# A four-layer graph network on one core: y's bank pair split by engine, layer 1's first maps placed behind the fourth chunk, and part of the fourth bank's sums put off

## The chip, the cores and the metric

The kernel runs on one core of one Trainium2 chip. The time is device microseconds for one execution. Three runs of the kernel before the change are known, and one more execution was taken by the hardware profiler. Engines are named as in the profile: PE is the matrix engine and PEld its weight loads, DVE the vector engine, ACT the scalar engine, POOL the general-purpose engine, and SP the engine that issues most transfers. All five have queues of their own[...].

## What is computed

The input x has 8 samples of 2048 nodes with 64 channels; adj is a 2048 x 2048 matrix. Four layers follow, each of the form "normalise, clamp at zero, run a graph layer, add to x":

```python
h = jnp.maximum(_layernorm(x, axis=-1), 0.0)
x = x + layer(h, adj)

# layer 0: three Chebyshev terms, weights of its own for every node
As = [I, A, 2 A @ A - I]
w = einsum('nd,dkio->nkio', embedding, weight)
out = einsum('bnki,nkio->bno', einsum('knm,bmc->bnkc', As, x), w) + embedding @ bias

# layer 1: three steps, node 0 of v replaced at the start
effects = einsum('nm,bmd->bnd', adj, v)
v = relu(concat([v, effects]) @ W1.T + b1) @ W2.T + b2

# layer 2: a weighted adj @ h, then a map.  layer 3: masked softmax attention over adj
```

Layer 0 is where y (its product with the node weights) is made, and layer 1's first step comes right behind it. These two places are what the change touches.

## The kernel before

**Data.** The main path (`uniform_path`) uses that every row of adj holds one value at its non-zero places: it keeps the signs as BT, 16 chunks of 128 nodes by 2048 columns, and multiplies the sums by a row of scales (`crow`). A float operand is split into a high part H (rounded) and a low part L (the rest), and a product with BT is two matmuls, one for each part, so 32 matmuls of 128x512 make one bank of 512 columns over all 16 chunks (`chunks`). There are four such banks (`NB`), and the 8 samples go in 4 pairs `p`. Layer 3's attention needs only sums in this path. A test of the matrix (`test`, `test_load`) runs beside layers 1: 64 pieces, each with a load `st`, a transposed load `mt` and one DVE operation `junk`, with three slots for the loads.

**The order of work.** Each engine's queue is fixed when the kernel is built. The kernel's `InOrder` wrapper ties the PE, and through layer 0's end and layer 1's first step all five engines, to the order in which the code issues; elsewhere a scheduler of the build places instructions by its own estimate of times. A tile of a pool comes free when the last reader of its former content is done.

**The y stage** (from line 1217, `apply_k`, `apply_w`, and the loop at line 1369) works through 16 groups `g` of 128 nodes. For each group the node weights are generated on the PE from the embedding E and the table wg (`make_w`, tiles `gen`, six steps of 16 matmuls, copied out by DVE and ACT in halves as `w<-gen`), and then applied to the three terms (`tt` holds the first two, `t2` or `t` the third) as matmuls of 32 columns into `yb`. In the loop step i of group g+1's `make_w` comes ahead of step i of group g's `apply_w`. Steps 0 to 2 of `apply_w` are the first half group (T = 0), steps 3 to 5 the second (T = 1). Step 0 or 3 applies the third term (`apply_k(.., 1)`), the two others the first two. A half group has two banks of sums, for the parities `par` of the output channels' halves. After step 2 or 5 they are copied to the tile `ys`; after step 5 four POOL transfers store `ys` to yD in memory. Beside it, in pieces, runs the normalisation for layer 1 of the first pair's first three blocks (`beside`).

The two banks of a half group are one tile `yb` of [128, 2, 512] with one buffer, and each of the two copies reads its half of the columns from both banks:

```python
for h in range(2):
    copy = (nc.scalar.copy, nc.vector.tensor_copy)[h]
    copy(to, yp[2].rearrange("p r (h x o) -> p h r x o", h=2, o=32)[:, h])
```

The last half group (g = 15, T = 1) takes two tiles of the pool `psg` instead, as `gen` tiles, and each engine then makes two copies of 256.

**Reload.** BT's room is used by the y stage, so 13 of its chunks (BT_A to BT_D) are loaded again at the stage's end as 16-bit values (`load_again`), and widened in place by ACT and DVE: `widen` copies the first half and the third quarter with the engine it is given, and the last quarter always with ACT. `by_act` names the chunks that ACT widens whole.

**Layer 1's first step** (`first_step`, line 1585) holds four banks of sums at once, in two tiles of two banks (`big`). In the first loop chunk m is added to all four banks, for m = 0 to 11, with H and L of the first three blocks (`H_u`, `L_u`). At m = 3 (`KEEP`) the last block (0,3) of the first pair gets its y added and is normalised (`x1_add`, `go_on`), with the widening of chunks 10 to 15 put between. At m = 8 `map_two(0)` is issued: eight matmuls `ph` from the tiles gT into two banks of the tag `tr`, whose four copies on ACT write gT back. After the loop the last block is transposed (`to_feat`: `pt_gT`, also of the tag `tr`), copied by ACT, mapped (`first_operand(3)`: `bn_u`) and split into H and L. Then each bank gets chunks 12 to 15 and is scaled by DVE (`scale`, result `g`), with `add` (a DVE add, a relu on ACT, two test pieces). In the third bank's turn come `map_two(2)` and `maps_two(0)` (`ph` and the 64 matmuls `bn`), the operand of the second step.

**Behind it**, in the second step, the blocks of the next pair are prepared through loads `acc`, `bn` (the bias), `yt` (the y of layer 0) on SP's queue, adds on DVE, a power (`rstd`) on POOL, stores `xs` and `hp` on POOL's queue. `acc` has two buffers; `sq` and `pl` share one.

Of the kernel before, what the change touches and what calls it, by code (L numbers as in the profile page):

```python
# [8 lines left out]
F32 = mybir.dt.float32  # L9
# [66 lines left out]
def uniform_path(  # L76
# [30 lines left out]
    nc = InOrder(tc)  # L107
    P = 128
    B, N, C = x.shape
    NP = B // 2  # L110
    NCH = N // P
    NB = N // 512
# [6 lines left out]
    psums = [pro.enter_context(tc.tile_pool(name="psump", bufs=1, space=bass.MemoryType.PSUM))]  # L119
# [11 lines left out]
    def bt(m):  # L131
        return BT[:, m] if m < KEEP else BTs[m - KEEP]
# [220 lines left out]
    def chunks(ps, hl, nb, ms, fill={}):  # L353
        for m in ms:
            for i in range(2):
                nc.tensor.matmul(
                    ps, hl[m // 4][i][:, m % 4, :], bt(m)[:, nb * 512:(nb + 1) * 512],
                    start=(m == 0 and i == 0), stop=(m == NCH - 1 and i == 1),
                )
            if m in fill:  # L360
                fill[m]()
# [271 lines left out]
    for m in range(NCH):  # L633
# [5 lines left out]
        if m % 2 and m < 12:  # L639
            k = m // 2 + 2  # L640
# [42 lines left out]
    for m in range(NCH):  # L683
# [14 lines left out]
        name="psumt", bufs=2, space=bass.MemoryType.PSUM, reuse_waits="tile"  # L698
# [127 lines left out]
    def first_operand(q):  # L826
        hl, gT = ops[0]
        hl.append(halves(back_whole(gT[q], w1e, f"u_{q}"), f"u_{q}"))
# [126 lines left out]
    def x1_load(p, nb):  # L955

        x1_rest(p, nb, *x1_first(p, nb))
# [19 lines left out]
    def x1_add(to=None):  # L977

        p, nb, acc, yt, bn = x1s.pop(0)
        nc.vector.tensor_tensor(  # L980
            nodes(acc), nodes(acc), bn[:, :, None, :].to_broadcast([P, 4, 2, C]), op=ALU.add
        )
        nc.vector.tensor_tensor(acc, acc, yt, op=ALU.add)
        keep(p, nb, acc, f"1_{p}_{nb}", b2r[:, None, None].to_broadcast([P, 4, 2, C]),
             lambda z, p, nb: to(z) if to else splits.append(lambda: store_planes(z, 1, p, nb)))
# [70 lines left out]
    for n, (kind, p) in enumerate(rounds):  # L1056
# [22 lines left out]
    hl = hl_of["b", 3]  # L1079
# [5 lines left out]
    psg = pgs.enter_context(tc.tile_pool(  # L1085
        name="psumg", bufs=4, space=bass.MemoryType.PSUM, reuse_waits="tile"
    ))
    psgs.append(psg)
    psl = pls.enter_context(tc.tile_pool(
        name="psuml", bufs=1, space=bass.MemoryType.PSUM, reuse_waits="tile"  # L1090
# [98 lines left out]
    for k in range(6):  # L1189
        make_w(0, k)  # L1190
        nb = 1 + k // 2
        for q in range(3 * (k % 2), 3 * (k % 2) + 3):
            m, i = order_l[NCH - KEEP + q // 2], q % 2
# [19 lines left out]
        name="psumy", bufs=1, space=bass.MemoryType.PSUM, reuse_waits="tile"  # L1213
# [3 lines left out]
    yps, yss = {}, {}  # L1217
# [29 lines left out]
    def apply_w(g, i):  # L1247

        T = i // 3
        if i in (0, 3):  # L1250
            if (g, T) == (NCH - 1, 1):
                yps[g, T] = [
                    psg.tile([P, 512], F32, tag="gen", name=f"yb_{g}_{T}_{par}") for par in range(2)
                ]
            else:
                yb = psums[-1].tile([P, 2, 512], F32, tag="yb", name=f"yb_{g}_{T}", bufs=1)
                yps[g, T] = [yb[:, 0], yb[:, 1], yb]
        u = 2 * T
        if i % 3 == 0:
            apply_k(g, u, 1)  # L1260
            apply_k(g, u + 1, 1)
        else:
            apply_k(g, u + i % 3 - 1, 0)
        if i in (2, 5):
            if T == 0:
                yss[g] = typ0.tile([P, 2, 4, 4 * C], F32, tag="ys", name=f"ys_{g}", bufs=2)
            ys, yp = yss[g], yps[g, T]
            for h in range(2):
                copy = (nc.scalar.copy, nc.vector.tensor_copy)[h]
                to = ys[:, h, 2 * T:2 * T + 2, :].rearrange("p s (j r o) -> p r (s j) o", j=4, r=2)  # L1270
                if len(yp) == 3:
                    copy(to, yp[2].rearrange("p r (h x o) -> p h r x o", h=2, o=32)[:, h])
                    continue
                for r in range(2):
                    copy(to[:, r], yp[r].rearrange("p (h x o) -> p h x o", h=2, o=32)[:, h])
            if T == 1:
                nb, t = divmod(g, 4)
                yr = ys.rearrange("(x j) h u f -> j x h u f", j=4)
                yd = yD[nb][:, :, :, t].rearrange("t b (j h u) c -> j (t b) h u c", h=2, j=4)
                for j in range(4):  # L1280
                    nc.gpsimd.dma_start(yd[j], yr[j][:, :, :, j * C:(j + 1) * C])
# [77 lines left out]

    shorts = {}  # L1360

    def widen(m, copy):

        to, src = shorts[m]
        for a, b in ((0, N // 2), (N // 2, 3 * N // 4)):
            copy(to[:, a:b], src[:, a:b])
        nc.scalar.copy(to[:, 3 * N // 4:], src[:, 3 * N // 4:])

    for g in range(NCH):
# [28 lines left out]
        name="psum", bufs=2, space=bass.MemoryType.PSUM, reuse_waits="tile"  # L1398
# [6 lines left out]
    for q in range(3):  # L1405
        first_operand(q)
    assert not splits
    by_act, by_dve = (3, 6, 9, 13), (4, 5, 7, 8, 10, 11, 12, 14, 15)
    for m in range(KEEP, 10):
        widen(m, nc.scalar.copy if m in by_act else nc.vector.tensor_copy)  # L1410

# [173 lines left out]
    def first_step(hl, gT, crow_of, g_new, hl_new, nm, map_two, maps_two, finish_two, scale, add):  # L1585

        two_ = [psums[-1].tile([P, 2, 512], F32, tag="big", name=f"bv2_{i}") for i in range(2)]
        sums = [two_[nb % 2][:, nb // 2] for nb in range(NB)]

        def crow(nb):  # L1590
            crow_of[nb] = load_crow(nb, f"{nm}_{nb}")

        crow(0)
        crow(1)
        for m in range(3 * NB):
            for nb in range(NB):
                chunks(sums[nb], hl, nb, (m,))
            if m == KEEP:
                x1_add(last_z.append)
                widen(10, nc.vector.tensor_copy)  # L1600
                go_on()
                widen(11, nc.vector.tensor_copy)
                go_on()
                for k in range(12, NCH):
                    widen(k, nc.scalar.copy if k in by_act else nc.vector.tensor_copy)
            if m == 2 * NB:
                map_two(0)
        ops[0][1].append(to_feat(last_z[0], feat(0, "gT_1_0_3"), "gT_1_0_3"))
        first_operand(3)
        x1_load(1, 0)  # L1610
        for _ in range(3):
            test_load()
        for nb in range(NB):
            chunks(sums[nb], hl, nb, range(3 * NB, NCH))
            scale(sums[nb], nb)
            if nb < 2:
                crow(nb + 2)
            if nb == 2:
                map_two(2)
                finish_two(0, maps_two(0))  # L1620
            add(nb)
            go_on()
        x1_load(1, 1)
        nc.on = ("gpsimd",)
        first_done.append(products[-1])
        later.extend((x1_behind, x1_behind))

        def put_off():
            ps = maps_two(2)
            return lambda: finish_two(2, ps)  # L1630

        carry.append(put_off)
        return hl_new, g_new
# [741 lines left out]
```

## Time and profile before

| | |
|---|---|
| time, median of three runs | 1145.01 us (1135.91, 1145.01, 1149.62) |
| the profiled execution | 1152.51 us, of which span 1150.4 us |
| mean granted PE clock | 0.972 |
| y stage, 291 to 505 us | PE busy 201.0 of 214.0 us, clock 0.97, DMA share 0.50 |
| 505 to 520 us | PE busy 11.0 of 15 us, clock 1.00, DMA share 0.75 |
| 530 to 545 us | PE busy 15.0 of 15 us, clock 1.00, DMA share 0.79 |
| 545 to 560 us | PE busy 10.4 of 15 us, clock 0.77, DMA share 0.08 |
| 590 to 605 us | PE busy 15.0 of 15 us, clock 1.00, DMA share 1.00 |
| 605 to 620 us | PE busy 9.3 of 15 us, clock 0.72, DMA share 0.88 |
| ACT's copies ys, 33 | 18.8 us busy |
| DVE's copies ys, 33 | 22.2 us busy |

All stretches are us from the span's start. A row of the profile gives line, engine, operation, output and input, count, busy time and mean duration, and then the idle time of the engine just before and what ended it. Since a wrapper issues every instruction, all of them have line 67, and one goes by the names of the tiles. In a timeline a line has start, length, engine, and in brackets the idle time before it with its releaser. A list of waits has total time, number and longest. The span has 1150.4 us; the DMA share is the mean busy share of the 16 DMA engines.

### The profile page before, as it was taken

The numbers are of one execution on the slowest core, as the hardware profiler recorded it, in microseconds if no ns is written. First come the engines' busy times: TensorE is split into PE (matmuls) and PEld (weight loads), VectorE is DVE, ScalarE is ACT, GpSimd is POOL, SyncE is SP. The second block draws the span as 40 slices with busy tenths as digits, with TensorE's granted clock in tenths as the row PEclk, the third lists the DMA queues.
The fourth block names the chain that finished last, engine by engine and source line by source line (L and its number), as shares of the span: only waits on it lengthen the run. The fifth ranks groups of instructions, "written<-read, shape, count | busy, mean of one in ns | idle before, by whom it ended". The sixth has DMA issues, their size and how long they took to land.

```text
span 1150.4 us, 28137 instructions
## 1 busy us (share of the span) xinstructions
PE 1078.9 (94%) x12030; PEld 865.6 (75%) x12030; DVE 642.6 (56%) x1193; ACT 435.9 (38%) x691; POOL 276.8 (24%) x313
## 2 busy tenths in 40 slices
PE   9999999999899999989898987999899999899996
PEld 7878778887788888877575765777577777688875
DVE  5555434412666667756485567547655644556575
ACT  5824422421455556545423432452244323211110
POOL 6514100100122323232022343133213300332121
PEclk9999999999999899999898998999899999899998
DMA  9936666555544454558488467736793662431432
GB/s 345 394 110 175 196 176 172 171 157 167 124 113 108 112 136 124 125 156 290 84 185 198 112 169 193 170 111 149 192 187 98 179 137 85 150 108 47 140 112 77
DMA packets 160198, 179.29 MB, mean 156 GB/s; under 512 B 63048, under 2 KB 114888, under 8 KB 157504
## 3 DMA queue, kind: packets, MB, share of 16 engines
q1 hardware_dynamic: 139744, 116.99, 41.0%
q0 software_dynamic: 13760, 45.21, 11.9%
q10 hardware_dynamic: 6560, 15.21, 4.0%
q8 instruction: 96, 1.57, 0.6%
q14 instruction: 38, 0.31, 0.1%
HBM read 111.81 MB, written 53.22 MB: 143 GB/s over the span
## 4 chain that ended last, share of the span: by engine, by line
PE 60%; DMA 12%; DVE 9%; issue 8%; ACT 4%; POOL 4%; SPq 3%; DVEq 0%; POOLq 0%; ACTq 0%
PE bv L67 22%; PE yb L67 7%; PE gen L67 6%; SPq L67 3%; PE bv_3a L67 3%; PE bv_2a L67 3%; PE bv_1a L67 2%; PE bv_2b L67 2%; PE bv_3b L67 2%; PE bn L67 2%; DMA yD<-ys 2%; PE bv_0a L67 2%; PE bv_1b L67 2%; DVE ys L67 2%; DMA yt<-yD 2%
## 5 line engine op out<-in xcount | busy, mean ns | idle before, releaser
L67 POOL TENSOR_TENSOR rstd<-var,mhalf 128x8 f32<-128x8 f32 x64 | 109.4, 1709 | 302.8 <-DVE var L67 300.1
L67 DVE COPY w<-gen 128x512 f32<-128x512 f32 x192 | 124.0, 687 | 57.0 <-PE gen L67 56.7
L67 ACT COPY w<-gen 128x512 f32<-128x512 f32 x192 | 104.7, 594 | 99.2 <-PE gen L67 98.4
L67 PE MATMUL gen<-E,wg 64*128 64x128 f32 (+1 forms) x1536 | 112.5, 287 | 1.8 <-issue 1.8
L67 ACT ACTIVATE sq<-z 128x512 f32<-128x512 f32 x64 | 40.5, 632 | 194.4 <-DVE z L67 147.2
L67 PEld LDWEIGHTS gen<-E,wg 64*128 64x128 f32 x1536 | 97.9, 192 | 19.6 <-issue 11.1
L67 PE MATMUL yb<-w,tt 128*32 128x128 f32 x2048 | 75.8, 288 | 4.8 <-issue 4.8
L67 POOL DMA_DIRECT2D yD<-ys x64 | 37.3, 590 | 166.6 <-DVE ys L67 164.9
L67 PE MATMUL bv<-BT_B,L 128*128 128x512 f32 x192 | 76.6, 399 | 0.2 <-DVE L L67 0.2
L67 PE MATMUL bv<-BT_C,H 128*128 128x512 f32 x192 | 76.8, 400 | 0.0
L67 PE MATMUL bv<-BT_B,H 128*128 128x512 f32 x192 | 76.5, 398 | 0.0
L67 PE MATMUL bv<-BT_C,L 128*128 128x512 f32 x192 | 75.3, 392 | 0.0
L67 DVE SCALAR_TENSOR_TENSOR z<-z,rstd 128x512 f32<-128x512 f32 x64 | 45.2, 706 | 52.8 <-POOL rstd L67 52.8
L67 PEld LDWEIGHTS yb<-w,tt 128*32 128x32 f32 x2048 | 60.8, 167 | 10.4 <-issue 5.7
L67 PE MATMUL bv<-BT,H 128*128 128x512 f32 x144 | 60.7, 422 | 3.8 <-ACT H L67 3.8
L67 DVE TENSOR_TENSOR g<-bv,crow 128x512 f32<-128x512 f32 x48 | 33.0, 688 | 55.9 <-PE bv L67 55.8
L67 PE MATMUL bv<-BT_A,L 128*128 128x512 f32 x144 | 58.0, 403 | 2.2 <-DVE L L67 2.2
L67 PE MATMUL bv<-BT,L 128*128 128x512 f32 x144 | 58.7, 408 | 1.0 <-DVE L L67 1.0
L67 PE MATMUL bv<-BT_A,H 128*128 128x512 f32 x144 | 57.7, 400 | 0.0
L67 DVE SCALAR_TENSOR_TENSOR junk<-mt,cols,st 128x512 uint8<-128x512 bf16 x64 | 47.8, 747 | 12.9 <-DMA mt<-MD 12.6
L67 POOL TENSOR_TENSOR acc<-acc,wl 128x512 f32<-128x512 f32 x16 | 23.4, 1463 | 126.1 <-DVE z L67 125.5
L67 PE MATMUL yb<-w,t 64*32 64x128 f32 x2048 | 41.0, 289 | 10.4 <-DVE ys L67 10.2
(271 smaller groups left out, 2398.0 us busy)
## 6 DMA issues: line engine op xcount, KB each, us to landing
BT<-in_adj_dram POOLq DMA_DIRECT2D x16, 1024.0 KB, 11.9
crow<-crowD SPq DMA_DIRECT2D x64, 256.0 KB, 3.8
st<-in_adj_dram SPq DMA_DIRECT2D x64, 256.0 KB, 4.2
MD<-md ACTq DMA_DIRECT2D x16, 512.0 KB, 4.0
tt<-TD SPq DMA_DIRECT2D x16, 512.0 KB, 4.5
t<-TD SPq DMA_DIRECT2D x32, 256.0 KB, 5.9
xs<-acc POOLq DMA_DIRECT2D x32, 256.0 KB, 3.1
acc<-xs SPq DMA_DIRECT2D x32, 256.0 KB, 3.4
```

What stands on the lines that cost most here:

```text
L67: made = f(*args, **how)
```

## The change

It has three parts. First, y's place: in place of one tile of two banks each half group has two tiles of one bank, one for each parity, and ACT copies the whole of the first, DVE the whole of the second; the last half group likewise, from `gen` tiles. Second, the first maps and the widening: `map_two(0)` goes from behind chunk 8 to behind chunk 3, ahead of the last block's normalisation; chunk 13 is widened by DVE; the last quarters of chunks 14 and 15 are widened behind `first_operand(3)`. Third, the fourth bank's sums of chunks 8 to 11 are left out of the first loop and made in its own turn.

```diff
@@ apply_w @@
         if i in (0, 3):
-            if (g, T) == (NCH - 1, 1):
-                yps[g, T] = [
-                    psg.tile([P, 512], F32, tag="gen", name=f"yb_{g}_{T}_{par}") for par in range(2)
-                ]
-            else:
-                yb = psums[-1].tile([P, 2, 512], F32, tag="yb", name=f"yb_{g}_{T}", bufs=1)
-                yps[g, T] = [yb[:, 0], yb[:, 1], yb]
+            yps[g, T] = [
+                psg.tile([P, 512], F32, tag="gen", name=f"yb_{g}_{T}_{par}", bufs=4)
+                if (g, T) == (NCH - 1, 1) else
+                psums[-1].tile([P, 512], F32, tag=f"yb{par}", name=f"yb_{g}_{T}_{par}", bufs=1)
+                for par in range(2)
+            ]
...
-            for h in range(2):
-                copy = (nc.scalar.copy, nc.vector.tensor_copy)[h]
-                to = ys[:, h, 2 * T:2 * T + 2, :].rearrange("p s (j r o) -> p r (s j) o", j=4, r=2)
-                if len(yp) == 3:
-                    copy(to, yp[2].rearrange("p r (h x o) -> p h r x o", h=2, o=32)[:, h])
-                    continue
-                for r in range(2):
-                    copy(to[:, r], yp[r].rearrange("p (h x o) -> p h x o", h=2, o=32)[:, h])
+            for par in range(2):
+                (nc.scalar.copy, nc.vector.tensor_copy)[par](
+                    ys[:, :, 2 * T:2 * T + 2, :].rearrange(
+                        "p h s (j r o) -> p h (s j) r o", j=4, r=2
+                    )[:, :, :, par],
+                    yp[par].rearrange("p (h x o) -> p h x o", h=2, o=32),
+                )
@@ widen @@
-    def widen(m, copy):
+    def widen(m, copy, whole=True):
 
         to, src = shorts[m]
         for a, b in ((0, N // 2), (N // 2, 3 * N // 4)):
             copy(to[:, a:b], src[:, a:b])
+        if whole:
+            widen_end(m)
+
+    def widen_end(m):
+        to, src = shorts[m]
         nc.scalar.copy(to[:, 3 * N // 4:], src[:, 3 * N // 4:])
...
-    by_act, by_dve = (3, 6, 9, 13), (4, 5, 7, 8, 10, 11, 12, 14, 15)
+    by_act = (3, 6, 9)
@@ first_step @@
         for m in range(3 * NB):
-            for nb in range(NB):
+            for nb in range(NB if m < 8 else NB - 1):
                 chunks(sums[nb], hl, nb, (m,))
             if m == KEEP:
+                map_two(0)
                 x1_add(last_z.append)
                 widen(10, nc.vector.tensor_copy)
                 go_on()
                 widen(11, nc.vector.tensor_copy)
                 go_on()
                 for k in range(12, NCH):
-                    widen(k, nc.scalar.copy if k in by_act else nc.vector.tensor_copy)
-            if m == 2 * NB:
-                map_two(0)
+                    widen(k, nc.vector.tensor_copy, k < 14)
         ops[0][1].append(to_feat(last_z[0], feat(0, "gT_1_0_3"), "gT_1_0_3"))
         first_operand(3)
+        widen_end(14)
+        widen_end(15)
...
         for nb in range(NB):
-            chunks(sums[nb], hl, nb, range(3 * NB, NCH))
+            chunks(sums[nb], hl, nb, range(3 * NB if nb < 3 else 8, NCH))
```

## The prediction

> **What bounds the kernel now.** I read the page's busy row first: the PE is busy 94% of the span, so what counts is where it stands still or runs slowly. Then, for the two places that the change touches, the list of waits of the y stage (291 to 520 us of the span) and the timelines of one half group and of layer 1's first step.
>
> ```profile
> PE 1078.9 (94%) x12030; PEld 865.6 (75%) x12030; DVE 642.6 (56%) x1193; ACT 435.9 (38%) x691; POOL 276.8 (24%) x313
> ```
>
> The waits of the y stage (total, times, longest):
>
> ```profile
> DVE ys L67 <- ACT ys L67: 39.6, 32, 4.8
> ACT ys L67 <- PE yb L67: 20.4, 25, 4.4
> PE yb L67 <- DVE ys L67: 10.2, 25, 1.4
> ```
>
> PE, ACT and DVE pass one baton: the last yb matmul, ACT's ys copy, DVE's ys copy, the next yb matmul. All 32 DVE copies wait for ACT's, and the PE pays 10.2 us. One half group, in order of time:
>
> ```profile
> 333.51 1.11 PE L67 MATMUL gen<-E,wg 64*128 64x128 f32 x16
> 333.64 0.58 ACT L67 COPY ys<-yb 128x512 f32<-128x512 f32 x1 [0.36 <-PE yb L67]
> 334.26 0.69 DVE L67 COPY ys<-yb 128x512 f32<-128x512 f32 x1 [0.90 <-ACT ys L67]
> 335.00 1.26 PE L67 MATMUL yb<-w,t 64*32 64x128 f32 x64 [0.38 <-DVE ys L67]
> 336.20 1.11 PE L67 MATMUL gen<-E,wg 64*128 64x128 f32 x16
> 337.24 1.14 PE L67 MATMUL yb<-w,tt 128*32 128x128 f32 x32
> ```
>
> With the baton, gen to yb takes 335.00 - 333.51 = 1.49 us; without it, 337.24 - 336.20 = 1.04. The difference, 0.45, is the loss. The second place:
>
> ```profile
> 542.96 2.88 ACT L67 CAST BT_C<-BT_C 128x512 fp32r<-128x512 bf16 x4 [2.23 <-DVE BT_C L67]
> 545.74 1.13 ACT L67 CAST BT_D<-BT_D 128x512 fp32r<-128x512 bf16 x2
> 546.78 2.36 ACT L67 COPY gT<-ph 64x512 f32<-64x512 f32 x4
> 548.59 0.66 PE L67 MATMUL pt_gT<-ident,z 128*128 128x128 f32 x4 [3.23 <-ACT gT L67]
> 549.92 1.84 PE L67 MATMUL bn_u<-w1e,gT 128*128 128x128 f32 x8 [0.68 <-ACT gT L67]
> 552.44 0.80 PE L67 MATMUL bv<-BT_C,H_u 128*128 128x512 f32 x1 [0.68 <-ACT H_u L67]
> ```
>
> The transposes of the last block need a bank of the maps' tag. The maps (ph) ran at 538.55, but ACT empties them only at 546.78, behind 4 us of widening. The PE stands 3.23 us, and the windows give 545 to 560 us a granted clock of 0.77 against 1.00 before.
>
> [...] after the 3.23 us stand bv matmuls start 0.43 us apart (554.18, 554.61), later 0.23. But the 2.53 us stand at 514.35 brought no slow spell. [...] the DMA share was 1.00 from 590 to 605 us, and a POOL store of 256 KB took about 8 us there, against a median of 3.1 on the page.
>
> **Part 1, y's place.** It removes two copies (33 + 33 become 32 + 32: the last half group has one copy per engine of 0.58 and 0.69 in place of two short ones) and the DVE-behind-ACT wait. The PE's order in this stage stays. New path from the last yb to the next: 0.04 + 0.69 (DVE, the slower) + 0.04 = 0.77 us, under the 1.04 to 1.08 of the 16 gen matmuls between: hidden with 0.27 to spare. 24 of the 25 stands go: 12 at about 0.45 and 12 at about 0.42 (326.51 to 328.01 is 1.50, 329.20 to 330.28 is 1.08), together 10.4; I take 10.3. The 25th is the last group's, with no gen beside it: its 1.43 us becomes about 0.8, -0.6. Sum **-10.9 us**. Low end: only the PE's own 10.2, less the 0.8 that stays, 9.4; high end: the weight loads' 14.2 us of waiting, less 0.8, 13.4. Late next would be the w<-gen copies, but DVE has about 4.6 us of copies in each half group of 6.5 (6 x 0.65 + 0.69), and gets to them earlier. POOL's yD stores now wait for both engines, both done sooner. At the end the stores leave some 0.4 us sooner still; I count nothing, since their landing stands behind the BT loads (DMA share 1.03 from 519 to 530); without that cover it is 0.4 of gain.
>
> **Part 2, maps and widening.** In the old profile's times: the maps' 8 matmuls (1.1 us on the PE) stay in amount; their four ACT copies (2.36) move into ACT's 4.37 idle us ahead of the square at 536.21. If that cover failed, the square and its norm would be up to 2.4 late. Chunk 13's first three quarters go from ACT to DVE: +1.1 there, between z (541.86) and chunk 14, so DVE ends its widening at 546.2 in place of 545.05, still ahead of L_u at 546.9. If not, L_u is later by the rest. The last quarters of 14 and 15 (1.13 on ACT) go behind H_u; only the fourth bank's last sums read them.
>
> **Part 3, sums put off.** 8 matmuls x 0.229 (the spacing 537.31 to 538.00 over three) = 1.83 us leave the first loop and come back in the fourth bank's turn. The loop ends at 545.2 - 1.8 = 543.4; z is ready, and the bank is free: no wait. Transposes to 544.1. ACT widens 13's last quarter when DVE is done at 544.05, then copies gT to 545.3; bn_u 1.0 (warm; 1.84 slow), H_u 0.6: first bv at 546.9, against 552.44. A warm clock saves 1.5 more in the first bank, whose product reaches DVE at 549.5 in place of 556.55: -7.0. From there to the third bank's product DVE's chain is the same 7.0 us (a test stands for its transposed load), so bn comes 7.0 earlier; the 8 sums return, +1.8. Parts 2 and 3: **-5.2 us** at the start of the second step. If the clock stays low -3.4; if the 0.7 us hand-overs shrink too -6.
>
> **What moves behind it.** The scheduler's order changes after this point. Six map matmuls of the second step go behind its first eight chunks (1.0 us, neutral). SP's loads change: the last bank's yt, crow and bias loads move a few places past the test loads, all of about 0.5 to 1.7 us of issue each and the same in number. On DVE one move matters: the bias add of block (1,3), which in before stood 2.77 us for acc<-in_x_dram at 609.17, moves some 4 us forward, ahead of the second step's third add. Queued behind it are that add and its relu on ACT, two tests (which free SP's test slots), the variances for POOL's two powers, the hp store, and the bn evacuation whose low halves the PE needs for step three. The load waits on SP for POOL's xs store of the block two before (issued 597.69, load issued 605.96). The trace does not show this order, so both ends: 0 if store and load come ahead, as SP's chain itself starts some 9 us earlier; +6 if the store takes its 8 us again. That stage already gave up 2.00 us at 610.52 and 3.37 at 617.36, which absorbs a part. I take **+2**, the delay of the low halves left after the stands that it replaces.
>
> **Sum.** -10.9 - 5.2 + 2 = -14.1. The profiled execution took 1152.51 us (span 1150.4, 2.1 around it), 7.5 above the median of the three runs; it goes to 1138.4, and the median 1145.0 to **1131 us**.
>
> **Rivals.** (a) Given back: the DVE stand costs its 6 us, or the clock stays low and it costs 4. For it: DMA share 1.00 there, and an 8 us store. Against: all of SP's chain is earlier. Total about -10 to -11: 1134. (b) The baton only changes names: with 0.27 us to spare, a norm piece on DVE (0.7 us each, in 10 of each four groups' 24 steps) or the gen banks hold the PE instead. Against: DVE is idle 0.9 us ahead of nearly every ys copy. Then part 1 gives about 3 and the rest 3: 1139. (c) Slower: the forward bias add turns into a long stand. Its place is the second step, its price one for one on the PE[...]. It decides from 16 us of cost on, a load landing some 13 us later than I put it. Against: no store or load in this window took over 9 us. With 22 us it ends at 1151. That the change doesn't do what it says is excluded for the waits, since the instruction order of the new kernel shows DVE's copies behind the PE alone.
>
> **Numbers.** Forecast 0.62, (a) 0.22, (b) 0.11, (c) 0.05. The likeliest case alone spans 1124 to 1137. One per cent, 11.5 us, is about what can be told from no change here: three runs of before lie 13.7 us apart. The range 1117 to 1143 takes the high end of part 1 with -6 and a few us of the runs' spread below, and (b) with the same spread above. Faster by over 1%: nearly 0.9 of the forecast and half of (a), 0.66; within 1% 0.28; slower 0.06, (c) and a little spread.
>
> **What would show it.** Right: no "DVE ys from ACT ys" in the waits, PE yb from ys under 1.5 us in all, half groups near 6.5 us; the stand before pt_gT gone and bn_u under 1.2 us; the first step's bv of bank one about 5 us closer behind the last yb. The bias add's stand on DVE before the third add, and the PE's before step three, tell the forecast from (a) and (c). Wrong: PE stands of 0.3 us or more named after gen or w; a slow clock after 545 all the same; more than 8 us of stand in step two.

## The result and the profile after

The changed kernel takes 1129.88 us (median of 4 runs, 1129.5 to 1138.15) against 1147.32 us of the kernel before (4 runs, 1135.91 to 1152.03): a ratio of 0.9878, interval 0.9831 to 0.9925. Its profiled execution took 1129.5 us, span 1127.4, against 1152.51 and 1150.4.

The page's busy row and, from the list of waits, the rows of the y stage after the change (total, times, longest):

```profile
PE 1071.0 (95%) x12030; PEld 861.4 (76%) x12030; DVE 645.3 (57%) x1194; ACT 434.2 (39%) x688; POOL 275.3 (24%) x313
```

```profile
DVE ys L67 <- PE yb L67: 16.1, 31, 3.4
ACT ys L67 <- PE yb L67: 8.1, 21, 1.9
...
PE yb L67 <- ACT ys L67: 0.5, 1, 0.5
...
PE gen L67 <- ACT ys L67: 0.3, 1, 0.3
```

The row "DVE ys from ACT ys" is gone, neither engine's copy waits for the other's, and of the PE's 10.2 us one stand of 0.5 is left, with one new stand of 0.3 before a gen matmul. The timeline of one half group:

```profile
336.93 0.59 ACT L67 COPY ys<-yb 128x512 f32<-128x512 f32 x1 [0.22 <-DVE w L67]
...
336.98 1.11 PE L67 MATMUL gen<-E,wg 64*128 64x128 f32 x16
...
337.16 0.69 DVE L67 COPY ys<-yb 128x512 f32<-128x512 f32 x1 [0.31 <-PE yb L67]
...
338.01 1.25 PE L67 MATMUL yb<-w,t 64*32 64x128 f32 x64
```

gen to yb takes 338.01 - 336.98 = 1.03 us, where the baton made it 1.49; the copies lie beside the gen matmuls. The third term's yb starts every 6.5 us (331.57, then 338.01).

Three marks cut the rest: the first bv of layer 1's first step, the first bv of the second step, and the third step's maps ph. Between the two profiles the way from the first yb to the first bv goes from 230.90 to 212.44 us (-18.5), the first step from 48.11 to 44.94 (-3.2), the second from 69.52 to 68.55 (-1.0), and what follows gives 0.4: 23.0 us of span. The second mark does not cut the two kernels at the same work: before, six map matmuls of the second step (1.01 us) run ahead of it, and after the change behind it. Like for like the first step gives 2.2 us and the second 2.0. The 23.0 us are more than the 17.4 between the medians. The windows of the two profiles at the same stretch say why (PE, PEld, DVE, ACT, POOL busy; clock; DMA share; GB/s), before first, after second:

```profile
365.00:395.00 30.00, 28.70 (x586) 24.78 (x588) 17.87 (x30) 15.00 (x28) 8.08 (x11) 0.77 0.39 91
```

```profile
365.00:395.00 30.00, 30.00 (x817) 26.82 (x810) 22.25 (x37) 20.37 (x39) 10.15 (x14) 1.00 0.55 135
```

The profile of before holds a spell at a clock of 0.77 in which two half groups took 9.37 and 11.21 us in place of 6.97. It is no part of the change. The kernel with parts 2 and 3 alone (below) has the old y stage without such a spell: 224.55 us. (Without its two long half groups the profile of before would have 224.3.) Against that, part 1 is worth 224.55 - 212.44 = 12.1 us, and the whole 12.1 + 3.2 + 1.0 + 0.4 = 16.7, near the medians' 17.4 and within the interval of the ratio, whose middle is 14.0. These are single executions: in the ten profiles with part 1, both engines copying and no such spell, the way is 210.67 to 214.76 us, mean 213.05, which makes part 1 worth 11.5 (9.8 to 13.9).

The place where the gain fell short is the first step, the timeline of PE, ACT and DVE after the change:

```profile
526.80 2.21 DVE L67 CAST BT_C<-BT_C 128x1024 fp32r<-128x1024 bf16 x4
527.03 0.63 PE L67 MATMUL pt_gT<-ident,z 128*128 128x128 f32 x4 [0.69 <-DVE z L67]
527.99 0.62 ACT L67 CAST BT_C<-BT_C 128x512 fp32r<-128x512 bf16 x1 [2.24 <-DVE BT_C L67]
...
529.05 0.62 ACT L67 CAST BT_C<-BT_C 128x512 fp32r<-128x512 bf16 x1 [0.44 <-DVE BT_C L67]
529.57 0.58 ACT L67 COPY gT<-pt_gT 128x512 f32<-128x512 f32 x1
530.20 1.16 PE L67 MATMUL bn_u<-w1e,gT 128*128 128x128 f32 x8 [2.55 <-ACT gT L67]
...
532.04 0.79 PE L67 MATMUL bv<-BT_C,H_u 128*128 128x512 f32 x1 [0.68 <-ACT H_u L67]
```

The 3.23 us stand before pt_gT is gone, but the PE now waits for z, and then 2.55 us for gT, which ACT copies only behind the last quarters of chunks 12 and 13; these wait for DVE, which is late because z was late. The bv behind it are 0.43 us apart again (533.36, 533.78).

### The profile page after: what moved, and what is told of

It is laid out like the page before. It is cut to its first block, busy times and chain, and to the rows that moved or that the text cites. A ratio compares the mean times of both kernels' runs of the same rounds, so it can differ in the third digit from the quotient of the medians.

```text
span 1127.4 us, 28157 instructions
## 1 busy us (share of the span) xinstructions
PE 1071.0 (95%) x12030; PEld 861.4 (76%) x12030; DVE 645.3 (57%) x1194; ACT 434.2 (39%) x688; POOL 275.3 (24%) x313
## 3 DMA queue, kind: packets, MB, share of 16 engines
q0 software_dynamic: 13760, 45.21, 11.8%
## 4 chain that ended last, share of the span: by engine, by line
PE 66%; DMA 11%; DVE 8%; issue 7%; POOL 3%; ACT 2%; SPq 1%; POOLq 0%; DVEq 0%; ACTq 0%
PE bv L67 26%; PE gen L67 9%; PE yb L67 9%; DMA BT<-in_adj_dram 2%; PE bv_3a L67 2%; PE bv_2b L67 2%; PE bv_3b L67 2%; PE bn L67 2%; PE bv_2a L67 2%; PE bv_1b L67 2%; PE bv_1a L67 2%; POOL rstd L67 2%; DVE z L67 2%; DMA xs<-acc 2%; SPq L67 1%
## 5 line engine op out<-in xcount | busy, mean ns | idle before, releaser
L67 PE MATMUL gen<-E,wg 64*128 64x128 f32 (+1 forms) x1536 | 109.4, 281 | 1.6 <-issue 1.4
L67 PEld LDWEIGHTS gen<-E,wg 64*128 64x128 f32 x1536 | 95.1, 186 | 18.4 <-issue 10.0
L67 PE MATMUL bv<-BT,H 128*128 128x512 f32 x144 | 61.9, 430 | 11.8 <-ACT H L67 10.6
L67 DVE SCALAR_TENSOR_TENSOR junk<-mt,cols,st 128x512 uint8<-128x512 bf16 x64 | 47.8, 747 | 10.6 <-DMA mt<-MD 10.2
L67 DVE SCALAR_TENSOR_TENSOR z<-mean,acc 128x256 f32<-128x256 f32 x112 | 49.2, 478 | 1.0
```

The lines of the kernel that those rows point to most:

```text
L67: made = f(*args, **how)
```

## The experiments

Theory: the PE's waits in the y stage were the baton, and the whole of it is won; the first step gains less than forecast because the last block's y comes with a block of loads that does not move along with the y stage. Rivals stand in each expectation. Each step length is that of one profiled execution, each time a median; the ratio is to the kernel before in the same series. In before, p1_only, p1_yt and no_putoff the six map matmuls (1.01 us) run ahead of the second step's first bv, in all others behind it, so by these marks the first step of those four is 1.0 us longer and the second 1.0 shorter.

| kernel | first yb to first bv | first step | second step to step three's maps | first BT_A load to add of y | time, us | ratio, interval |
|---|---|---|---|---|---|---|
| before | 230.90 (with the spell) | 48.11 | 69.52 | 24.7 | 1147.32 | |
| changed | 212.44 | 44.94 | 68.55 | 25.0 | 1129.88 | 0.9878, 0.9831 to 0.9925 |
| p1_only | 211.56 | 52.83 | 69.35 | 25.1 | 1138.88 | 0.9952, 0.9927 to 0.9976 |
| p23_only | 224.55 | 43.13 | 64.90 | 24.8 | 1139.68 | 0.9948, 0.9926 to 0.9970 |
| both_dve | 218.63 | 42.35 | 68.69 | 24.6 | 1134.73 | 0.9930, 0.9895 to 0.9966 |
| ends_behind | 212.47 | 45.65 | 67.70 | 24.7 | 1130.18 | 0.9877, 0.9817 to 0.9938 |
| yt_first | 212.49 | 45.31 | 67.92 | 22.4 | 1129.46 | 0.9829, 0.9775 to 0.9884 |
| bias_tied | 214.76 | 49.30 | 63.37 | 24.8 | 1132.27 | 0.9860, 0.9804 to 0.9917 |
| no_putoff | 213.85 | 46.69 | 69.86 | 24.6 | 1132.64 | 0.9859, 0.9805 to 0.9913 |
| yt_ends | 213.09 | 41.16 | 67.42 | 22.0 | 1126.34 | 0.9825, 0.9763 to 0.9887 |
| after_again | 210.67 | 47.15 | 68.27 | 24.7 | 1136.76 | 0.9897, 0.9842 to 0.9953 |
| warm_fill | 219.71 (clock 0.97) | 45.48 | 66.38 | 25.0 | 1131.44 | 0.9842, 0.9781 to 0.9902 |
| all_three | 214.57 | 43.12 | 68.27 | 22.2 | 1129.59 | 0.9837, 0.9774 to 0.9901 |
| p1_yt | 214.64 | 45.99 | 67.50 | 22.3 | 1136.82 | 0.9909, 0.9872 to 0.9945 |

How far one execution can be trusted is shown by three of these rows. In the first step the changed kernel, after_again and bias_tied have the same matmuls in the same order (bias_tied's edit lies behind it), and the step took 44.94, 47.15 and 49.30 us. They start bn_u at nearly the same point, 26.89, 26.24 and 26.87 us after the first bv (mean 26.7). From there to the second step they took 18.05, 20.91 and 22.43 us at a granted clock of 0.91, 0.76 and 0.70. So the start of bn_u can be compared between kernels, and a difference of 2 us in the step's length, from one execution of each, cannot.

**p1_only: part 1 alone.** The kernel before with the two hunks of `apply_w`.

> The kernel before with part 1 alone (y's two tiles of one bank, one copy engine each). The forecast's theory: from the first yb matmul to the last the y stage takes about 209 us, as with the whole change (208.7), half groups of 6.5 us, no wait of DVE's ys copies for ACT's; layer 1's first step keeps its stand before pt_gT. Then the time is about 11 us under the kernel before (8 to 13). Rival, the loads set the end: the reload of BT and the last y load do not come earlier along with the y stage, so the last block's y lands some 19 us behind the last ys copy in place of 15, its z is 3 to 4 us later against the first bv, and the way from the first bv of the first step to the second step's first bv grows from 48.1 to about 51; then the time is only about 7 us lower.

The y stage did what the forecast said, but the first step grew by 4.7 us, more than the rival's 3, and the time fell by only 0.5%. The PE's line before the last block's transposes:

```profile
534.59 1.11 PE L67 MATMUL pt_gT<-ident,z 128*128 128x128 f32 x4 [6.79 <-ACT gT L67]
```

The stand doubled from 3.23 to 6.79 us. Only about half of the y stage's 12 us reached the end (6.7 by the medians, 5.5 by the ratio): the rival holds.

**p23_only: parts 2 and 3 alone.** The kernel before with all other hunks.

> The kernel before with parts 2 and 3 alone (maps behind chunk 3, widening of 13 to 15 moved, eight sums put off). With the whole change the way from the first step's first bv to the second step's was 44.9 us in place of 48.1, 3.2 less, where the forecast had 5.2. If the missing 2 us come from part 1 (a shorter y stage leaves the loads behind), this kernel has the old y stage, its last y lands about 15 us behind the last ys copy, no stand before bn_u over 1.3 us, and the way is about 43 us: the forecast's size. Rival: the missing 2 us are made in the step itself (ACT's last quarters of chunks 12 and 13 ahead of its copy of gT): then bn_u waits 2 us or more here as well and the way is 45. Time against the kernel before: 3 to 6 us lower, the second step's bias-add stand of about 5 us on DVE included.

The first step takes 43.13 us, 5.0 less than before (4.0 like for like): near the forecast's size, and the time is 5.9 us under the kernel before. bn_u waited 1.01 us and started 23.08 us after the first bv, against 28.06 before. (The profiled execution is the fastest of the twenty, 1131.33 us, so its later stretches are not typical.) The y stage of before, in a second execution of it, shows these waits:

```profile
DVE ys L67 <- ACT ys L67: 37.8, 32, 4.6
...
PE yb L67 <- DVE ys L67: 11.7, 29, 1.4
```

There are 29 stands of 31 half groups, where the profile of before listed 25. And the loads, first here and then in the changed kernel (the POOL store hp, its transposed load, the reloads, the last y and its add):

```profile
496.75 0.71 POOL L67 DMA_DIRECT2D hp<-pl  x1 [5.50 <-ACT pl L67]
...
499.32 2.57 SPq L67 DMA_TRANSPOSE pt<-hp  x2
...
502.00 1.47 SPq L67 DMA_DIRECT2D BT_A<-MD  x3
...
526.84 0.69 DVE L67 TENSOR_TENSOR acc<-acc,yt 128x512 f32<-128x512 f32 x1 [5.36 <-DMA yt<-yD]
```

```profile
488.68 0.71 POOL L67 DMA_DIRECT2D hp<-pl  x1 [6.40 <-ACT pl L67]
...
491.48 2.45 SPq L67 DMA_TRANSPOSE pt<-hp  x2
...
494.04 3.16 SPq L67 DMA_DIRECT2D BT_A<-MD  x3
...
519.00 0.69 DVE L67 TENSOR_TENSOR acc<-acc,yt 128x512 f32<-128x512 f32 x1 [7.88 <-DMA yt<-yD]
```

From the first BT_A load to the add of y it is 24.8 us in one and 25.0 in the other. The first BT_A load, behind the transposed load of the block before on SP's queue, came 8.0 us earlier (502.00 to 494.04), the first bv 11.7 (514.98 to 503.31). The 3.7 us that the y stage gained behind that load never reached y. The DMA share over the block is 0.96 in one and 0.98 in the other, which left next to no room to land sooner. Most of the 3.7 us are two stands of the old y stage, here in p23_only:

```profile
502.60 1.26 PE L67 MATMUL yb<-w,t 64*32 64x128 f32 x64 [1.43 <-DVE ys L67]
...
510.00 1.57 PE L67 MATMUL yb<-w,tt 128*32 128x128 f32 x47 [2.28 <-issue]
```

The first, the last group's, fell to 0.48 us in the changed kernel. The second, at the very last yb and named "issue", is gone there; the forecast had no term for it.

**both_dve: one engine makes both copies** of a half group.

```diff
-                (nc.scalar.copy, nc.vector.tensor_copy)[par](
+                nc.vector.tensor_copy(
```

> The changed kernel, but DVE makes both ys copies of a half group, one behind the other. If part 1 works because the copies' path gets shorter than the 16 gen matmuls beside it (1.06 us), then 2 x 0.69 + 0.08 = 1.46 us sticks out by 0.4 us in each of 31 half groups: half groups of 6.9 us, yb matmuls wait for ys about 12 us in all, the y stage 221 us in place of 208.7, and the time is about that of the kernel before less 5. Rival: what cost was two engines meeting in one bank (the hand-over from ACT to DVE), not the length: then one engine and two banks keep half groups at 6.5 us and the time stays near 1130.

Both numbers missed: the half group is 6.71 us long (the median; 6.97 with the old y stage, 6.54 in the changed kernel), between the two.

```profile
331.47 1.29 DVE L67 COPY ys<-yb 128x512 f32<-128x512 f32 x2
...
331.55 1.11 PE L67 MATMUL gen<-E,wg 64*128 64x128 f32 x16
...
332.59 1.46 PE L67 MATMUL yb<-w,t 64*32 64x128 f32 x64
...
333.98 1.11 PE L67 MATMUL gen<-E,wg 64*128 64x128 f32 x16
```

Two copies behind one another take 1.29 us, not 1.38, and yb starts on time, 1.04 us after gen: its first matmul needs only the first tile, and starts 0.17 us ahead of the end of the second copy (332.59 against 331.47 + 1.29). What is paid is inside: to the next gen it takes 1.39 us, against 1.18 in the changed kernel (331.57 to 332.75 there). So one engine with two banks wins about three fifths of the half group's 0.43 us, and the rest is lost again when both copies lie behind one another. The first step, behind a longer y stage, takes 42.35 us: y's add comes 12.9 us after the first bv, in place of 15.7. So the time, 1134.73, lies between the two expectations too.

**ends_behind: chunks 12 and 13's last quarters behind the operand too.**

```diff
-                    widen(k, nc.vector.tensor_copy, k < 14)
+                    widen(k, nc.vector.tensor_copy, False)
...
-        widen_end(14)
-        widen_end(15)
+        for k in range(12, NCH):
+            widen_end(k)
```

> The changed kernel, but the last quarters of chunks 12 and 13 too are widened behind the last block's operand (only the fourth bank's last sums read them). If ACT's copy of gT is late because these two quarters stand ahead of it and wait for DVE, the copy starts right behind the transposes: bn_u waits about 0.7 us in place of 2.55, the matmuls behind it stay at 0.23 us each, and the second step starts 2 to 3.5 us earlier against the first bv (42 to 43 us in place of 44.9). Rival: DVE's widening of chunks 14 and 15 or the split behind bn_u is what comes next and holds L_u: then the first bv gains, but the bank's product does not, and the second step starts within 1 us of 44.9. Time 0 to 4 us under the changed kernel.

```profile
527.93 1.16 PE L67 MATMUL bn_u<-w1e,gT 128*128 128x128 f32 x8 [0.68 <-ACT gT L67]
529.77 0.51 PE L67 MATMUL bv<-BT_C,H_u 128*128 128x512 f32 x1 [0.68 <-ACT H_u L67]
531.39 0.56 PE L67 MATMUL bv<-BT_C,L_u 128*128 128x512 f32 x1 [1.11 <-DVE L_u L67]
```

bn_u came 2.1 us earlier (24.8 after the first bv in place of 26.9), as the theory has it, but L_u then waited for DVE's widening and eight bv followed one another 0.40 to 0.43 us apart. The step, 45.65 us, lies among those of the changed kernel's code. The rival named what came next.

**yt_first: the last y ahead of BT_D.**

```diff
             load_again("C", 4)
-            load_again("D", 2)
             x1_rest(0, NB - 1, *firsts_.pop(0))
+            load_again("D", 2)
```

> The changed kernel, but the last block's y is loaded ahead of BT_D (two chunks, 1 MB) in place of behind it. If the block of loads sets when the last block gets its y (from the first BT_A load to the add of y it was 24.6 to 25.1 us in each of the six traces so far, wherever the y stage ended), the add comes about 2.5 us earlier: some 22.5 us after the first BT_A load, 13.2 us after the first bv in place of 15.7; z too, and the PE no longer waits for BT_C or z there. The second step then starts 2 to 4 us earlier against the first bv (41 to 43 us in place of 44.9), time 1126 to 1128. Rival: y's own way through memory (the stores of the last group, issued at 501.2, then the load) sets it: the load is issued 2 us earlier but waits for these stores, the add moves by less than 1 us and the second step stays at 44 to 45.

The block's length was as expected (22.4 us; y's add 13.2 us after the first bv), so the load's place in the block sets it and not the stores of yD. bn_u started 24.42 us after the first bv, though ACT's copy of gT still stood behind the two quarters (2.37 us before bn_u). The step's length, 45.31, shows nothing of that gain: the clock from there to the maps was 0.71 (bn_u took 2.08 us, against 1.16 in the changed kernel).

**yt_ends: the two together.**

> The changed kernel with both: the last block's y loaded ahead of BT_D, and the last quarters of chunks 12 and 13 widened behind the last block's operand. Alone the second edit brought bn_u 2.1 us forward but left the second step where it was, since L_u then waited 1.1 us behind DVE's widening, with a slow clock after it. If z comes 2.5 us earlier, DVE's widening is over earlier too, L_u no longer waits for it, and both edits add: bn_u 22 to 23 us after the first bv in place of 26.9, the second step at 40 to 42 in place of 44.9, time 1124 to 1127. Rival: the fourth bank's end, ACT's copies behind the maps (2 us of stand before ph) or the slow clock take it back: second step within 1 us of the better of the two edits alone.

41.16 us, within the expectation. bn_u starts 22.74 us after the first bv, 3.9 ahead of the changed code's mean of 26.7, where the two edits alone gave 1.8 and 2.2: at this point the gains add. L_u no longer waits as in ends_behind (0.22 us against 1.11), and no bv behind it is slow (0.23 us apart from 529.58 up to the maps):

```profile
526.68 1.16 PE L67 MATMUL bn_u<-w1e,gT 128*128 128x128 f32 x8 [0.67 <-ACT gT L67]
528.52 0.50 PE L67 MATMUL bv<-BT_C,H_u 128*128 128x512 f32 x1 [0.68 <-ACT H_u L67]
529.24 0.51 PE L67 MATMUL bv<-BT_C,L_u 128*128 128x512 f32 x1 [0.22 <-DVE L_u L67]
```

**p1_yt: part 1 with the y ahead of BT_D**, the same edit on p1_only.

> Part 1 alone, with the last block's y loaded ahead of BT_D as well. Part 1 alone made the first step 52.8 us long in place of 48.1, with a stand of 6.8 us before pt_gT where the kernel before has 3.2. If that loss is the block of loads, which the shorter end of the y stage no longer covers, y's add comes 2.5 us earlier, the stand before pt_gT shrinks to about 4.3, and the first step takes 49 to 50.5 us; time about 2.5 us under part 1 alone (1136 against 1138.9, or a ratio of 0.992 to 0.994 in place of 0.995). Rival: what holds the transposes is ACT's own work of widening and map copies, not when z comes; then the stand stays over 6 us and the step at 52 to 53.

The stand before pt_gT fell from 6.79 to 2.67 us and the step to 45.99, more than expected. bn_u started 27.49 us after the first bv, against 32.32 in p1_only. Some 1.6 us of these 4.8 are this execution's own: its first BT_A load stood 10.8 us ahead of the first bv, against 9.2 in p1_only. Another 2.0 us of the step lie behind bn_u, where the granted clock was 0.83 against 0.72. What is left is about the theory's size: with the load's place alone changed, y came 2.7 us earlier behind the block's start, and the stand shrank with it. In the times the intervals of p1_yt (0.9909) and p1_only (0.9952) overlap.

**no_putoff: the eight sums back in the first loop.**

```diff
-            for nb in range(NB if m < 8 else NB - 1):
+            for nb in range(NB):
...
-            chunks(sums[nb], hl, nb, range(3 * NB if nb < 3 else 8, NCH))
+            chunks(sums[nb], hl, nb, range(3 * NB, NCH))
```

> The changed kernel, but all four banks take chunks 0 to 11 in the first loop, so no sums are put off (the bias add of block (1,3) then falls back to its old place, behind the third add). Theory from the traces: with the whole change the loop ends before z is there and the PE waits 0.7 us for z and 2.55 for gT, so the eight matmuls (1.83 us) that were put off only made room for these waits and come back later in the fourth bank. With them in the loop, bn_u starts at the same point (26.9 us after the first bv), and the second step 1.5 to 2 us earlier (43.0 to 43.5 in place of 44.9), with a warm clock up to 3.5 us earlier. Rival: as the forecast put it, the loop's end holds the transposes and bn_u: then bn_u is 1.8 us later and the second step starts at the same point (44.5 to 45.5).

bn_u started 26.6 us after the first bv, no later than with the sums put off: in the changed kernel the loop's end holds nothing. The step did not get shorter, though. Behind a 2.61 us stand eleven bv followed one another 0.43 us apart, and the second step started at 46.7, of which 1.0 are the six map matmuls that run ahead of the mark here. What the put-off sums cost or give in the whole change is not settled by this; with y on time (p23_only) there was no wait left for them to cover.

**bias_tied: the bias add of (1,3) behind the third add again.**

```diff
         if ahead_x:
-            x1_add()
+            with tc.issue_after(gadds[2]) if n == 0 and st == 1 else nullcontext():
+                x1_add()
```

> The changed kernel, but block (1,3)'s bias add on DVE is tied behind the second step's third add, its place in the kernel before. The forecast's theory: the forward place costs (it took 2 us for it, after the stands it replaces); then the 4.9 us stand on DVE no longer holds the third add, the PE's 5.4 us stand before step three shrinks, and from the second step's start to the third step's first maps it is 2 us less or more: 66.5 or under in place of 68.55. Rival: the stand only changes its owner, because the load behind the store is late either way and what waits for it, the operand of step three, comes out of the same DVE queue; the stands of the kernel before there (2.0 and 3.4 us) come back and the stretch is 68 to 69.5, the time unchanged within 1 us.

In the changed kernel the forward add did stand, and the third add and the PE with it:

```profile
584.60 0.69 DVE L67 TENSOR_TENSOR acc<-acc,bn 128x512 f32<-128x512 f32 x1 [4.91 <-DMA acc<-in_x_dram]
585.21 0.69 DVE L67 TENSOR_TENSOR g<-g,g 128x512 f32<-128x512 f32 x1
...
589.05 0.80 PE L67 MATMUL bv<-BT,H 128*128 128x512 f32 x1 [5.37 <-ACT H L67]
```

Tied, the stretch fell to 63.37 us in this profile, more than the theory asked for, but the first step of the same execution took 49.30. The two together are 112.67 us, against 113.49 in the changed kernel, and the time did not fall (1132.27).

**all_three: yt_ends and bias_tied in one.**

> The changed kernel with the three edits together: the last block's y loaded ahead of BT_D, the last quarters of chunks 12 and 13 behind the last block's operand, the bias add of block (1,3) behind the third add. If each removes its own stand, the first step takes about 41 us (44.9) and the second step's stretch to the third step's maps 62 to 64.5 (68.55), and the time is 1119 to 1124, 6 to 10 us under the changed kernel. Rival: what the second step gives is taken back by later stands (tied alone, the bias add saved 5.2 us in its stretch and nothing in the time), and the time is 1125 to 1128, like the first two edits alone.

With the add in its old place the stretch is 68.27 us here, and these are the stands in it, on DVE and on the PE:

```profile
595.99 0.69 DVE L67 TENSOR_TENSOR acc<-acc,yt 128x512 f32<-128x512 f32 x1 [2.61 <-DMA yt<-yD]
```

```profile
597.14 1.13 PE L67 MATMUL bn<-wl,g 64*64 64x64 f32 x32 [5.43 <-ACT g L67]
```

DVE stands for the next block's y, and the PE before the maps bn, as in the kernel before (3.37 us there). Over all profiles the stretch is 63.4 to 69.9 us with the add in its old place (six of them, mean 68.0, and 68.7 with the six map matmuls counted in all) and 64.9 to 68.7 in the forward one (eight, mean 67.5). No cost of the forward place can be told from this; there is a stand in either. The time of all_three, 1129.59 us, is 7.2 under the changed kernel in the same series, but by its ratio it is no better than yt_ends, and the second step of 62 to 64.5 us that was expected did not come. The lowest ratios are those of yt_ends, yt_first and all_three (0.9825, 0.9829, 0.9837). Their intervals overlap that of the changed kernel (0.9878), so that they beat it is not shown.

**after_again and warm_fill: the same code once more, and the PE kept busy.**

```diff
         ops[0][1].append(to_feat(last_z[0], feat(0, "gT_1_0_3"), "gT_1_0_3"))
+        keep_warm("tr", 11)
         first_operand(3)
```

> The changed kernel once more, beside the two below. Both theories: 1129 to 1132, about 14 to 17 us under the kernel before. It shows how much of a profile's differences come from one execution: the forecast's steps should stay (y stage 206 to 208 us from the first yb to the last, the last block's y about 25 us behind the first BT_A load, first step 44 to 47 depending on whether the clock falls behind the 2.5 us stand).

> The changed kernel with 11 matmuls of no use (about 0.21 us each, 2.3 in all) put on the PE between the transposes of the last block and bn_u, where it waits 2.55 us for gT; nothing else moves. Theory: behind that stand the clock falls for 2 to 3.5 us (bv matmuls 0.43 us apart in place of 0.23), in some executions more, which is why the first step takes 44.9 us in one profile and 49.3 in another of the same code; with the PE kept busy bn_u starts at the same point, the bv matmuls stay at 0.23, and the first step takes 43 to 44 us; time 1 to 3 us under the changed kernel. Rival: the clock follows something else (the weak stretch ahead of it, the waits for BT_C and z), the slow matmuls stay, and the first step is at 44.5 to 49.

After_again took 1136.76 us, above the expectation, with 2.2 us more in the first step for the same stand; its ratio (0.9897) agrees with the first measurement. The maps' line in the changed kernel, bn_u and the maps in after_again, then warm_fill:

```profile
543.32 1.23 PE L67 MATMUL bn<-wl,g 64*64 64x64 f32 x64
```

```profile
529.45 2.07 PE L67 MATMUL bn_u<-w1e,gT 128*128 128x128 f32 x8 [2.54 <-ACT gT L67]
...
543.90 2.74 PE L67 MATMUL bn<-wl,g 64*64 64x64 f32 x64
```

```profile
541.69 0.50 PE L67 MATMUL bv<-BT_C,H_u 128*128 128x512 f32 x1 [0.67 <-ACT H_u L67]
...
551.04 1.13 PE L67 MATMUL ph<-g,wl 64*64 64x512 f32 x2 [2.05 <-ACT gT L67]
551.92 1.98 PE L67 MATMUL bn<-wl,g 64*64 64x64 f32 x64
```

With the PE busy no bv ran slowly (0.23 us apart from the third on), where all three executions without the filling have bv 0.42 to 0.43 us apart behind the stand of 2.54 or 2.55 us: in these four executions the slow bv come with the stand. The expected 43 to 44 us were missed, and 45.48 lies among the steps without filling. The slow matmuls came at the next stand, 2.05 us before the maps, and these took 1.98 us. That the filling moved them there is not shown: the maps took 1.23 us in one execution without it, but 2.74 in after_again and 2.58 in bias_tied.

## Why the prediction was right, and where not

**The total.** 1131 was forecast, 1129.88 came; the ratio puts the gain at 8.6 to 19.4 us, the forecast had 14.1. That it came so near is in part luck, because two errors cancel. By the times, part 1 alone took off 5.5 us (2.7 to 8.4) in place of 10.9, and parts 2 and 3 alone, with what moves behind them, 6.0 (3.4 to 8.5) in place of 3.2. The two together make 11.5, and the whole change was measured twice, at 14.0 and 11.8: within the noise the parts add.

**Part 1, -10.9 us.** In the y stage itself 12.1 was measured (11.5 against the mean of ten), within the range given (9.4 to 13.4), and in the way named: the DVE-behind-ACT wait gone, the path under the gen matmuls, 6.5 us for a half group. That two tiles would end this wait was the author's estimate; the traces show 32 such waits before (39.6 us) and none after. Why DVE waited for ACT on the one tile was not shown. The count in "24 of the 25 stands go" was low: in p23_only 29 stands cost the PE 11.7 us, of which 0.8 is left. That makes 10.9, the forecast's own sum; the stands named "issue" account for 0.8 of the rest (4.8 us in p23_only, 4.0 after). The last group's stand became 0.48, where 0.8 was said. That the copies might hold the PE elsewhere (rival b) is excluded: only stands of 0.5 and 0.3 us are left. What was mis-sized is how much of the y stage's gain reaches the end: all of it was counted, and by the time of p1_only about half came, mainly for the reason in the next paragraph.

**Parts 2 and 3, -5.2 us.** Alone 5.0 (p23_only; 4.0 like for like). In the whole change the first step is 3.2 us shorter in one execution, 1.0 in the second (47.15), and 1.2 longer in the third with the same code there (49.30). The step that failed is "z is ready" at the loop's end, which the forecast put at 543.4. It left z where the old profile had it, while part 1 drew the first bv nearer to a block of loads of 25 us that starts at a place inside the y stage. The remark that the stores' landing stands behind the BT loads held the reason, and was used only to count a gain at nothing, not for the loss: y's add comes 15.7 us after the first bv in place of 12.1. With z late, DVE's casts and ACT's quarters were late too, and in place of a copy of gT right behind the transposes came the 2.55 us stand. Late y costs the first step 4.7 us without parts 2 and 3 (52.83 against 48.11) and 1.8, 4.0 and 6.2 with them (44.94, 47.15 and 49.30 against 43.13), 4.0 in the mean. At the start of bn_u, ahead of the slow clock, it is 4.3 without them and 3.6 with them. So part 1 gives back some 4 us here with or without parts 2 and 3, and these are worth about as much as alone; the forecast had no term for this loss. That part 1 alone gives only 0.5% in time agrees.

**What moves behind, +2 us.** The stand came, of 4.91 us, near the upper end of the 0 to 6 given, but the stretch got 1.0 us shorter (2.0 like for like), and bias_tied with all_three show no cost of the place itself. What was mis-sized is the delay net of the stands replaced: the old place has stands of the same kind, 3.2 to 5.8 us before the maps bn. Rival (a)'s stand was there without its price; rival (c) needed a load 13 us later than it came.

**The clock.** "A warm clock saves 1.5 more in the first bank" held only in part: behind a stand of 2.55 us the bv came 0.42 to 0.43 us apart in place of 0.23, and from bn_u to the second step the granted clock was 0.91, 0.76 and 0.70 in three executions.

## What to carry to other kernels

When a stage gets shorter, look for the transfers that start inside it and are waited for behind it: here only the gain made ahead of their start was passed on (8.0 of 11.7 us, p23_only against the changed kernel); the other 3.7 us never reached y, and a new wait of 2.55 us came. Two banks in two tiles freed two engines of each other here (32 waits of DVE for ACT, 39.6 us, before and none after), and even a single copying engine gained (6.71 us for a half group against 6.97), because the next matmul needs only the first tile (it started 0.17 us ahead of the second copy's end). Before a difference of a step is explained, see how far executions of the same code lie apart: here 44.94 to 49.30 us for one step, by the granted clock, while the mark ahead of the slow clock, the start of bn_u, moved by 0.7. By that mark the two edits behind the late y gave 1.8 and 2.2 us alone and 3.9 together.

## What was not expected of the hardware

- The block of loads is the steadiest length here: 24.6 to 25.1 us from the first BT_A load to the add of y in ten traces, 22.0 to 22.4 in the four where 1 MB comes behind y. The DMA share over it was 0.97 before, 0.96 in p23_only and 0.98 in the changed kernel.
- The clock. Behind the same stand (2.55 and 2.54 us) bn_u took 1.16 us in one execution of the changed kernel and 2.07 in the other. Behind the next one (2.04 and 2.05 us) the maps took 1.23 us in the changed kernel and 1.98 in warm_fill; whether the shorter stands ahead of it, 0.7 us each, count in was not shown. In all_three, stands of 0.68, 0.68 and 0.64 us close together were followed by seven bv 0.43 us apart.
- With the old y stage, the profiles have a stand of 2.3 to 2.5 us named "issue" at the very last yb (2.53 before, 2.28 in p23_only), and both_dve has one of 1.62. With one copy on each engine it is 1.03 in p1_yt, 0.48 in yt_ends and absent in the nine others. It was not tried what makes it. A part of the 12.1 us of part 1 is this stand, and since it lies behind the start of the loads, so is a part of what y came late by.
